# The opening of a two-layer image kernel: order of the first loads, statistics per chunk, and extra TensorE products

## The chip, the cores and the metric

The kernel runs on one core of a Trainium2 chip. The metric is the device time of one execution in microseconds (us); the median of the runs counts. A core has a matrix engine (TensorE, PE in the profile), a vector engine (VectorE, DVE), a scalar engine (ScalarE, ACT), a general engine (GpSimd, POOL) and a queue engine that issues transfers (SyncE, SP). They run side by side and wait for each other by semaphores. Products are written to PSUM banks; all else lies in SBUF, 128 partitions wide.

## What is computed

Two images of 768 channels and 64 x 64 pixels pass through two layers, each with a residual. Each begins with a group norm over 32 groups of 24 channels. The first layer is a state-space block: a projection to 1536 channels, a 3 x 3 convolution per channel, SiLU, a scan over the 4096 pixels, a norm over channels, a projection back. The second is an attention-like block with two projections.

```python
def _gn(v, G=32, eps=1e-5):
    B_, C_, H_, W_ = v.shape
    g = v.reshape(B_, G, C_ // G, H_, W_)
    m = jnp.mean(g, axis=(2, 3, 4), keepdims=True)
    s = jnp.var(g, axis=(2, 3, 4), keepdims=True)
    return ((g - m) / jnp.sqrt(s + eps)).reshape(v.shape)
...
x = x + _L0_conv_ref(_gn(x), ...)
x = x + _L1_conv_ref(_gn(x), L1_conv_W_qkv, L1_conv_W_out, L1_conv_temp)
```

The change touches the group norms, above all that of image 0, with which the kernel begins. All data are float32.

## The kernel before, in words

The order of the instructions of each engine is written out by hand (`manual_schedule`); an engine executes its own in that order, and SP issues its transfers in order too, so that one that waits holds up all behind it.

**The opening (L1156 to L1180).** The constants are issued first: `ident` (L1492), `pc`, `comb`, `xsum` (L80 to L84). Then image 0 is loaded in 48 pieces of 128 channels x 512 pixels, 256 KB each (`gn_load`, L149), and DVE takes the statistics of each (`bn_stats`, L154). Six chunks of 128 channels have eight pieces each; `gn_aggregate` (L231) joins them into a mean and a variance per channel after the last piece.

The channels of a group lie in different partitions, so `gn_parts` joins them on PE. `average` (L188) multiplies the six chunks by six averaging matrices of 128 x 32 and adds up in PSUM: one value per group. `groups` (L193) copies it out, `spread_groups` (L198) multiplies it by six selecting matrices of 32 x 128, one for each chunk: back to one value per channel. This is done twice, for the means and for the variances about them (`deviations`, L204 to L207, between), then `variance` and `end` form the scale (L210 to L214) and `then` the bias (L237, L238). The averaging matrices (`gavg_in`, L170) and the selecting ones (`gsel_in`, L176, two transfers) are loaded into tiles taken from a list of free tiles, `slots`, served in order (`take`, `give`).

The same functions serve image 1 (run in the main loop), and layer 1's group norms of both images (`gn_next`): parts of image 0's stand in the main loop, those of image 1's in the product phase of layer 1 (`beside`), where the weights are loaded by L876 and multiplied by L886.

Behind the statistics of image 0, SP issues: the two matrices, the first tile of x (L307, six), the weights of the first `in_proj` (L323), a first row of x (L337), two more weights, 24 pieces of image 1, `xp_w`, `dt_w`, `pick`. When the scale is there, DVE norms the row (`norm_x0`, L341) and ACT the tile (`norm_x`, L317).

**The filling.** Then come 16 steps. Step n computes on PE, in the first twelve, one row of 64 pixels (`row0`, L348, six products of 128 x 64), and in all 512 pixels (`in_proj`, L362, six products of 128 x 512) for a block of 128 of the 1536 channels, with a weight block (L323) loaded two steps ahead; there are four weight tiles. ACT copies the row out (`carry`, L349) and the rest (`in_proj_evict`, L374 to L377) to one of two buffers `xs`, which DVE reads two steps later for the convolution (`taps_dve`, L461). `row0` writes a PSUM bank of which there is one (`pz`), so it waits until ACT has copied the row before out (L349). ACT writes a buffer `xs` only after DVE has read what was in it. In the same steps DVE takes the statistics of the last 24 pieces of image 1 (`xg`). The taps of the first block stand on DVE behind the first two of those.

**After it** the main loop of 192 steps runs the scan on DVE beside `in_proj` and `out_proj` (L603) on PE, and layer 1 follows.

PE's first product (`acc_mark`, L135) writes the bank `acc` once from `ident` and a zeroed buffer.

Of the kernel before, what the change touches and what calls it, by code (L numbers as in the profile page):

```python
# [7 lines left out]
F32 = mybir.dt.float32  # L8
AF = mybir.ActivationFunctionType
ALU = mybir.AluOpType  # L10
# [4 lines left out]
P = 128  # L15
NB, DM, H, W = 2, 768, 64, 64
L = H * W
# [4 lines left out]
KM = DM // P  # L22
KI = DI // P
G = 32
GC = DM // G
HEADS = 12
HD = DM // HEADS
EPS = 1e-5


TR = 8
# [26 lines left out]
N_MORE = 33  # L58

N_TAIL = 4 * KM  # L60


XD2 = 64
# [2 lines left out]

@with_exitstack
def both_layers(
    ctx, tc, nc, consts, x, in_wP, xp_wP, dt_wP, out_wT, pc_in, comb_in, pick_in, xsum_in, gavg_in, gsel_in, wo_dr, bc_dr, s_dr, x1, stats1,
    qkvP, woutP, temp_c, hcol_in, hsel_in, esel_in, out  # L70
):
    ident, ones, eps_c = consts

    wp = ctx.enter_context(tc.tile_pool(name="l0w", bufs=1))

# [1 line left out]
    r0 = right.enter_context(tc.tile_pool(name="l0r", bufs=1, side="right"))  # L77

    pc = wp.tile([P, KI, PC_N], F32, name="pc")
    nc.sync.dma_start(pc, pc_in)  # L80
    comb = wp.tile([P, 2, P], F32, name="comb")
    nc.sync.dma_start(comb, comb_in)
    xsum = r0.tile([P, XM], F32, name="xsum")
    nc.sync.dma_start(xsum, xsum_in)  # L84
    xp_w = r0.tile([P, KI, XD2], F32, name="xp_w")
    dt_w = r0.tile([XM, KI // 2, P], F32, name="dt_w")
    neg_a = r0.tile([P, KI, NS], F32, name="neg_a")
# [3 lines left out]

    xv = [x[b].rearrange("(k p) h w -> p k (h w)", p=P) for b in range(NB)]
    gp = ctx.enter_context(tc.tile_pool(name="l0gn", bufs=1))
    st_in = [gp.tile([P, KM, L // 512, 6], F32, name="st_in")] * NB
    mv_in = [gp.tile([P, KM, 2], F32, name=f"mv_in{b}") for b in range(NB)]

# [15 lines left out]
    def take():  # L112
        return slots.pop(0)
# [17 lines left out]
    psS = ctx.enter_context(tc.tile_pool(name="l0_pss", bufs=1, space=PSUM))  # L131


    acc = psC.tile([P, 512], F32, tag="acc", name="acc_mark")
    nc.tensor.matmul(acc, ident, xs_bufs[0][:, :TR, :W], start=True, stop=True)  # L135


    pieces = {}
# [3 lines left out]
    def gn_load(b, v):  # L142
        k, h = divmod(v, L // 512)
        if v < N_EARLY[b]:
            pieces[b, v] = take()
        else:
            tag, bufs = (("delta", 3), ("sq", 3), ("du", 2))[v % 8 // 3]
            pieces[b, v] = wk.tile([P, 512], F32, tag=tag, name=f"xg{b}_{v}", bufs=bufs)
        nc.sync.dma_start(pieces[b, v], xv[b][:, k, h * 512 : (h + 1) * 512])  # L149

    def gn_piece(b, v):
        k, h = divmod(v, L // 512)
        piece = pieces.pop((b, v))
        nc.vector.bn_stats(st_in[b][:, k, h, :], piece)  # L154
        if v < N_EARLY[b]:
            give(piece)

    def gn_parts(name, mv, mean, rstd, then, keep=False):

        st, held = {}, {"avg": [], "sel": []}

        def load(what):
            if what in st:
                return
            if what == "avg":
                held["avg"] = [take()]
                st["avg"] = held["avg"][0][:, : KM * G].rearrange("p (k g) -> p k g", g=G)
                nc.sync.dma_start(st["avg"], gavg_in)  # L170
            else:
                held["sel"] = [take(), take()]
                st["sel"] = []
                for h, t in enumerate(held["sel"]):
                    t = t[:G, : KM // 2 * P].rearrange("g (k p) -> g k p", p=P)
                    nc.sync.dma_start(t, gsel_in[:, h * (KM // 2) : (h + 1) * (KM // 2), :])  # L176
                    st["sel"] += [t[:, k, :] for k in range(KM // 2)]

        def done(what):
            if not keep:  # L180
                st.pop(what)
                for t in held[what]:
                    give(t)

        def average(src):
            st["ps"] = psZ.tile([P, 512], F32, tag="pz", name=f"pg_{name}")
            for k in range(KM):
                nc.tensor.matmul(st["ps"][:G, 0:1], st["avg"][:, k, :], src[:, k : k + 1], start=(k == 0), stop=(k == KM - 1))  # L188
            done("avg")

        def groups():
            st["gs"] = gp.tile([G, 1], F32, tag="gn_g", name=f"gs_{name}")
            nc.vector.tensor_copy(st["gs"], st["ps"][:G, 0:1])  # L193

        def spread_groups():
            st["ps"] = psZ.tile([P, 512], F32, tag="pz", name=f"pb_{name}")
            for k in range(KM):
                nc.tensor.matmul(st["ps"][:, k : k + 1], st["sel"][k], st["gs"], start=True, stop=True)  # L198
            done("sel")

        d = gp.tile([P, KM], F32, tag="gn_d", name=f"d_{name}")

        def deviations():
            nc.vector.tensor_copy(mean, st["ps"][:, :KM])  # L204
            nc.vector.tensor_sub(d, mv[:, :, 0], mean)
            nc.vector.tensor_mul(d, d, d)
            nc.vector.tensor_add(d, d, mv[:, :, 1])  # L207

        def variance():
            nc.vector.tensor_scalar_add(d, st["ps"][:, :KM], EPS)  # L210
            nc.scalar.activation(d, d, AF.Sqrt)

        def end():
            nc.vector.reciprocal(rstd, d)  # L214
            then()
            if keep:
                for t in held["avg"] + held["sel"]:
                    give(t)

        nothing = lambda: None  # L220
        return [
            (lambda: load("avg"), lambda: average(mv[:, :, 0]), groups),
            (lambda: load("sel"), spread_groups, deviations),
            (lambda: load("avg"), lambda: average(d), groups),
            (lambda: load("sel"), spread_groups, variance),
            (nothing, nothing, end),
        ]

    def gn_aggregate(b):
        for k in range(KM):  # L230
            nc.vector.bn_aggr(mv_in[b][:, k, :], st_in[b][:, k, :, :])  # L231

    def gn_finish(b):
        mean = gp.tile([P, KM], F32, name=f"xmean{b}")

        def then():
            nc.vector.tensor_mul(xbias[b], mean, xscale[b])  # L237
            nc.vector.tensor_scalar_mul(xbias[b], xbias[b], -1.0)  # L238
            nc.vector.tensor_scalar_mul(stats1[b][:, :, 2 * NT], mv_in[b][:, :, 0], -1.0)

        return gn_parts(f"x{b}", mv_in[b], mean, xscale[b], then, keep=(b == 0))
# [79 lines left out]
    def load_wi(n):  # L321
        w = take_w(KM)
        nc.sync.dma_start(w, in_wP[n % KI])  # L323
        wis[n] = w
# [14 lines left out]
    def norm_x0():  # L339
        for k in range(KM):  # L340
            nc.vector.tensor_scalar(  # L341
                x0s[0][:, k, :], x0s[0][:, k, :], xscale[0][:, k : k + 1], xbias[0][:, k : k + 1], ALU.mult, ALU.add
            )
# [811 lines left out]
    with tc.manual_schedule():  # L1155
        for v in range(N_PIECE):  # L1156
            gn_load(0, v)
            gn_piece(0, v)
        gn_aggregate(0)
        parts = gn_finish(0)  # L1160
        for load, pe, dve in parts[:2]:
            load()
# [3 lines left out]
        load_x0()  # L1166
        for n in (1, 2):
            load_wi(n)
        for v in range(N_EARLY[1]):
            gn_load(1, v)  # L1170
        nc.sync.dma_start(xp_w, xp_wP)
        nc.sync.dma_start(dt_w, dt_wP)
        for load, pe, dve in parts:
            pe()
            dve()
        norm_x0()
        for k in range(KM):
            norm_x(0, k)
# [300 lines left out]

@with_exitstack  # L1480
def mamba_then_attention(
    ctx, tc, x, in_wP, xp_wP, dt_wP, out_wT, pc_in, comb_in, pick_in, xsum_in, qkvP, woutP, temp_c, ident_in, gavg_in, gsel_in, hcol_in, hsel_in, esel_in, out
):
    nc = tc.nc
    keep = ctx.enter_context(tc.tile_pool(name="keep", bufs=1))
    dram = ctx.enter_context(tc.tile_pool(name="dram", bufs=1, space=DRAM))
    x1 = [dram.tile([DM, L], F32, name=f"x1_{b}") for b in range(NB)]

    stats1 = [keep.tile([P, KM, 2 * NT + 1], F32, name=f"stats1_{b}") for b in range(NB)]

    ident = keep.tile([P, P], F32, name="ident")
    nc.sync.dma_start(ident, ident_in)  # L1492
    ones = keep.tile([P, P], F32, name="ones")
    nc.vector.memset(ones, 1.0)
    eps_c = keep.tile([P, 1], F32, name="eps_c")
    nc.vector.memset(eps_c, EPS)
    consts = (ident, ones, eps_c)


    wo_dr = dram.tile([KM // 2, KI // 3, P, 3, 2 * P], F32, name="wo_dr")  # L1500
    bc_dr = [dram.tile([2 * NS, TL], F32, name=f"bc_dr{i}") for i in range(NI)]

    s_dr = {k: dram.tile([KM // 2, 4, P, KM // 2, P], F32, name=f"s_dr_{k}") for k in ("p1", "p3")}
    both_layers(
        tc, nc, consts, x, in_wP, xp_wP, dt_wP, out_wT, pc_in, comb_in, pick_in, xsum_in, gavg_in, gsel_in, wo_dr, bc_dr, s_dr, x1, stats1,
        qkvP, woutP, temp_c, hcol_in, hsel_in, esel_in, [out[b].rearrange("c h w -> c (h w)") for b in range(NB)],
    )

# [104 lines left out]
```

## Time and profile before

| | us |
|---|---|
| median of three runs | 3709.17 |
| lowest, highest | 3702.92, 3709.97 |
| span of the profiled execution | 3708.1 |
| PE busy in it | 3555.3 (96%) |
| DVE busy | 2842.1 (77%) |
| ACT busy | 2571.8 (69%) |
| POOL busy | 1782.8 (48%) |

Of the profiled execution the span is known, from its first instruction to its last; the median of the timed runs is 1.07 us above it. The profile lists instructions by engine with their line in the kernel, the tile that is written and those that are read, and what ended the idle time ahead of each. PE is the matrix engine's products, PEld its loads of weights, SPq the issues of transfers. Times in the timeline are counted from the span's start.

### The profile page before, as it was taken

To read this page: it belongs to the slowest core of one execution; us is meant where nothing else is said; L and a number is where in the kernel's file an instruction comes from. 1 tells how busy PE (TensorE), PEld (TensorE's weight loads), DVE (VectorE), ACT (ScalarE), POOL (GpSimd) and SP (SyncE) were. 2 spreads that over 40 slices of the span, in tenths; PEclk is the share of its full clock that TensorE was granted. 3 is DMA by queue.
4 is the path that set the end of the run, shared out by engine and by line. 5 is a ranking of instruction groups with operands and counts; after the bars stand their busy time and mean duration, and the time that the engine had idled before them with its cause. 6 is when DMAs were issued, how large, how long until landed. Compare 5 with 4: busy or idle time off the path is not lost. (4 is left out here: it accounts for less than half of the span.)

```text
span 3708.1 us, 37935 instructions
## 1 busy us (share of the span) xinstructions
PE 3555.3 (96%) x11176; PEld 1771.0 (48%) x11176; DVE 2842.1 (77%) x2571; ACT 2571.8 (69%) x5026; POOL 1782.8 (48%) x1813
## 2 busy tenths in 40 slices
PE   5968999999999999999999999999999999999999
PEld 3423333343333333333344333433347658886688
DVE  7899999999999999999999999997721362224522
ACT  2688889888988898888888988897633542244221
POOL 0355565565655655555556655654443313330232
PEclk9978999999999999999999999999999999999999
DMA  9877888998989899898898989997676538763487
GB/s 354 232 169 162 182 204 185 205 211 191 212 176 209 201 200 208 184 204 185 187 203 194 212 175 211 203 201 177 142 202 183 192 93 265 256 205 123 158 268 245
DMA packets 380301, 738.98 MB, mean 199 GB/s; under 512 B 44304, under 2 KB 116944, under 8 KB 376000
## 3 DMA queue, kind: packets, MB, share of 16 engines
q0 software_dynamic: 146208, 270.08, 42.6%
q1 hardware_dynamic: 233888, 466.49, 38.4%
q8 instruction: 90, 1.47, 0.2%
q14 instruction: 115, 0.94, 0.1%
HBM read 440.96 MB, written 60.03 MB: 135 GB/s over the span
## 5 line engine op out<-in xcount | busy, mean ns | idle before, releaser
L362 PE MATMUL pa<-u,w 128*128 128x512 f32 (+1 forms) x2304 | 1035.8, 599 | 7.5 <-ACT carry L377 7.3
L603 PE MATMUL po<-u,w 128*128 128x512 f32 x2256 | 1011.5, 598 | 8.1 <-DVE u L615 7.9
L539 DVE TENSOR_TENSOR_SCAN s<-da,s 128x2052 f32<-128x2052 f32 x192 | 851.1, 4433 | 19.5 <-DVE s L537 0.9
L362 PEld LDWEIGHTS pa<-u,w 128*128 128x128 f32 x2304 | 429.5, 192 | 597.7 <-issue 484.7
L603 PEld LDWEIGHTS po<-u,w 128*128 128x128 f32 x2256 | 420.8, 190 | 582.7 <-issue 551.3
L526 POOL TENSOR_TENSOR ysum<-da 128x1024 f32<-128x1024 f32 x192 | 386.8, 2015 | 547.4 <-DVE da L546 464.1
L461 DVE SCALAR_TENSOR_TENSOR acc<-xs,pc,acc 128x512 f32<-128x512 f32 x698 | 525.6, 753 | 29.2 <-ACT acc L415 12.7
L537 DVE TENSOR_TENSOR s<-du,bc 128x2048 f32<-128x2048 f32 x192 | 439.2, 2288 | 83.0 <-POOL du L518 73.8
L433 POOL DMA_DIRECT2D tm<-tm x309 | 270.3, 875 | 462.7 <-ACT tm L427 423.5
L514 ACT ACTIVATE da<-dl,neg_a 128x512 f32<-128x512 f32 x768 | 489.6, 713 | 0.0
L546 DVE TENSOR_TENSOR da<-s,bc 128x2048 f32<-128x2048 f32 x192 | 440.0, 2292 | 6.3
L533 POOL DMA_DIRECT2D u<-ysum x384 | 380.4, 1255 | 4.2 <-issue 3.5
L427 ACT ACTIVATE tm<-xs,pc 128x512 f32<-128x512 f32 x486 | 317.1, 717 | 15.1 <-DMA tm<-tm 7.3
L415 ACT ACTIVATE acc<-xs,pc 128x512 f32<-128x512 f32 x192 | 132.2, 688 | 215.7 <-DVE u L461 206.4
L518 POOL TENSOR_TENSOR du<-dl,u 128x512 f32<-128x512 f32 x192 | 246.5, 1284 | 0.0
L439 POOL DMA_DIRECT2D u<-tm x177 | 206.1, 1164 | 59.6 <-issue 50.1
L447 PE MATMUL acc<-xs,dg 128*128 128x512 f32 x264 | 140.0, 641 | 50.0 <-ACT acc L415 49.6
L886 PE MATMUL po_p<-v,w 128*128 128x256 f32 x672 | 171.9, 380 | 1.4 <-ACT po_p L983 1.4
L886 PE MATMUL po_p<-u,w 128*128 128x256 f32 x624 | 159.7, 379 | 0.0
L461 DVE SCALAR_TENSOR_TENSOR u<-xs,pc,acc 128x512 f32<-128x512 f32 x192 | 143.6, 748 | 7.7
L831 POOL TENSOR_TENSOR v<-u 128x256 f32<-128x256 f32 x21 | 15.7, 758 | 277.1 <-ACT u L849 262.1
L886 PE MATMUL acc_p<-u,w 128*128 128x256 f32 x556 | 143.7, 382 | 4.6 <-DMA w<-woutP 3.4
(285 smaller groups left out, 5006.5 us busy)
## 6 DMA issues: line engine op xcount, KB each, us to landing
u<-ysum POOLq DMA_DIRECT2D x384, 256.0 KB, 5.5
tm<-tm POOLq DMA_DIRECT2D x309, 256.0 KB, 4.3
w<-in_wP SPq DMA_DIRECT2D x192, 384.0 KB, 4.4
w<-wo_dr SPq DMA_DIRECT2D x192, 384.0 KB, 4.7
u<-x SPq DMA_DIRECT2D x263, 256.0 KB, 4.8
w<-s_dr_p SPq DMA_DIRECT2D x288, 192.0 KB, 3.4
u<-tm POOLq DMA_DIRECT2D x177, 256.0 KB, 5.8
bc<-bc_dr SPq DMA_DIRECT2D x32, 1024.0 KB, 7.7
```

The lines of the kernel that those rows point to most:

```text
L362: nc.tensor.matmul(pa[:, :nn], w[:, k, :], xts[i, k][:, :nn], start=(k == 0), stop=(k == KM - 1))
L427: nc.scalar.activation(tm.rearrange("p (h w) -> p h w", w=W), xs[:, dy : dy + TR, dx : dx + W], AF.Copy, scale=pc[:, c, PC_W + j : PC_W + ...
L433: nc.gpsimd.dma_start(tms[a][0], tms[a][q], accum_op=ALU.add)
L461: nc.vector.scalar_tensor_tensor(dst, xs[:, dy : dy + TR, dx : dx + W], pc[:, c, PC_W + j : PC_W + j + 1], acc, ALU.mult, ALU.add)
L514: nc.scalar.activation(das[g % 2][:, n, 1:], deltas[g], AF.Exp, scale=neg_a[:, c, n : n + 1])
L526: nc.gpsimd.tensor_add(ysum[:, 0 : 2 + g % 2 : 1 + g % 2, :], da[:, 0:2, 1:], da[:, 2:4, 1:])
L533: nc.gpsimd.dma_start(us[g], ysums(g, n), accum_op=ALU.add)
L537: nc.vector.tensor_mul(s[:, :, 1:], dus.pop(g).unsqueeze(1).to_broadcast([P, NS, TL]), bc[:, :NS, :])
L539: nc.vector.tensor_tensor_scan(sf, das[g % 2].rearrange("p n l -> p (n l)"), sf, 0.0, ALU.mult, ALU.add)
L546: nc.vector.tensor_mul(das[g % 2][:, :, 1:], s[:, :, 1:], bc[:, NS:, :])
L603: nc.tensor.matmul(po[e], w[:, kk, e * P : (e + 1) * P], us[i * KI + k], start=(k == 0), stop=(k == KI - 1))
L886: nc.tensor.matmul(dst, half[:, k, :], tiles[blocks[seq[i][0]][:3]][what][k], start=(start and k == 0), stop=(k == KH - 1), skip_group_che ...
```

## The change

1. The four constants leave the front of SP's queue. `ident` and `comb`, and a new one, `ghalf` (32 x 2), are issued behind the ninth piece; `pc` behind the weights of the first three steps; `xsum` behind the 24 pieces of image 1.
2. Each chunk of image 0 is aggregated as soon as its eighth piece has its statistics.
3. PE gets products whose result nobody reads: `warm` multiplies `ident` by `comb` (128 x 256) into the bank `acc`; `warm_behind` does so behind a product that reads the statistics of one of the last ten pieces of image 0. One more `warm` stands behind the first spread, two behind the second, and `mark`, the former first product, behind the last part of the norm.
4. A value per group is spread by three matrices of 32 x 128 instead of six: the channel chunks k and k+3 have the same pattern, with groups shifted by 16, so a moving operand of two columns (`ghalf` masks one half of the groups in each) gives both. One transfer of `gsel_in` instead of two, one tile taken instead of two. This holds for all four group norms.
5. The bias of layer 0's norms is one instruction instead of two.

```diff
+    def warm(n=1):
+        acc = psC.tile([P, 512], F32, tag="acc", name="acc_warm")
+        for _ in range(n):
+            nc.tensor.matmul(acc[:, : 2 * P], ident, comb.rearrange("p e m -> p (e m)"), start=True, stop=True)
+
+    def warm_behind(b, k, h):
+        acc = psC.tile([P, 512], F32, tag="acc", name="acc_behind")
+        nc.tensor.matmul(acc[:, :6], ident, st_in[b][:, k, h, :], start=True, stop=True)
+        warm()
+
+    def mark():
+        acc = psC.tile([P, 512], F32, tag="acc", name="acc_mark")
+        nc.tensor.matmul(acc, ident, xs_bufs[0][:, :TR, :W], start=True, stop=True)
...
-                held["sel"] = [take(), take()]
...
+                held["sel"] = [take()]
+                st["sel"] = held["sel"][0][:G, : KM // 2 * P].rearrange("g (k p) -> g k p", p=P)
+                nc.sync.dma_start(st["sel"], gsel_in)
...
-            nc.vector.tensor_copy(st["gs"], st["ps"][:G, 0:1])
+            st["gs"] = gp.tile([G, 2], F32, tag="gn_g", name=f"gs_{name}")
+            nc.vector.tensor_mul(st["gs"], st["ps"][:G, 0:1].to_broadcast([G, 2]), ghalf)
...
-            for k in range(KM):
-                nc.tensor.matmul(st["ps"][:, k : k + 1], st["sel"][k], st["gs"], start=True, stop=True)
+            for k in range(KM // 2):
+                nc.tensor.matmul(st["ps"][:, 2 * k : 2 * k + 2], st["sel"][:, k, :], st["gs"], start=True, stop=True)
...
-            nc.vector.tensor_copy(mean, st["ps"][:, :KM])
+            nc.vector.tensor_copy(chunks(mean), by_chunk())
...
-            nc.vector.tensor_scalar_add(d, st["ps"][:, :KM], EPS)
+            nc.vector.tensor_scalar_add(chunks(d), by_chunk(), EPS)
...
-            nc.vector.tensor_mul(xbias[b], mean, xscale[b])
-            nc.vector.tensor_scalar_mul(xbias[b], xbias[b], -1.0)
+            nc.vector.scalar_tensor_tensor(xbias[b], mean, -1.0, xscale[b], ALU.mult, ALU.mult)
...
         for v in range(N_PIECE):
             gn_load(0, v)
+            if v == 8:
+                nc.sync.dma_start(ident, ident_in)
+                nc.sync.dma_start(comb, comb_in)
+                nc.sync.dma_start(ghalf, ghalf_in)
             gn_piece(0, v)
-        gn_aggregate(0)
+            k, h = divmod(v, L // 512)
+            if h == L // 512 - 1:
+                nc.vector.bn_aggr(mv_in[0][:, k, :], st_in[0][:, k, :, :])
+            if v >= N_PIECE - N_WARM:
+                warm_behind(0, k, h)
...
+        nc.sync.dma_start(pc, pc_in)
         for v in range(N_EARLY[1]):
             gn_load(1, v)
+        nc.sync.dma_start(xsum, xsum_in)
         nc.sync.dma_start(xp_w, xp_wP)
         nc.sync.dma_start(dt_w, dt_wP)
-        for load, pe, dve in parts:
+        for q, (load, pe, dve) in enumerate(parts):
             pe()
+            warm((0, 1, 0, 2, 0)[q])
             dve()
+        mark()
         norm_x0()
```

## The prediction

> **What bounds the kernel.** The table by engine came first (PE 3555.3 of 3708.1 us), then the timeline of the first 90 us, where nearly all of the change lies, then the three later group norms. fp32 products are recorded as two instructions each ("halves"), so x12 is six products. In the timeline (start, duration, engine, line, operation, count, idle before it and what ended that):
>
> ```profile
> 2.59 31.19 SPq L149 DMA_DIRECT2D u<-x  x48
> 39.26 0.69 DVE L154 BATCH_NORM_STATS2 st_in<-u 128x6 f32<-128x512 f32 x1 [0.42 <-DMA u<-x]
> 39.87 1.51 DVE L231 BATCH_NORM_AGGREGATE mv_in<-st_in 128x2 f32<-128x48 f32 x6
> 41.93 2.72 PE L198 MATMUL pb_x<-gs_x,u 32*128 32x1 f32 x12 [0.24 <-DVE gs_x L193]
> 45.60 0.77 PE L188 MATMUL pg_x<-d_x,u 128*32 128x1 f32 x12 [0.95 <-DVE d_x L207]
> 50.84 2.79 PE L348 MATMUL pa<-u,w 128*128 128x64 f32 x12 [1.52 <-issue]
> 53.43 6.74 PE L362 MATMUL pa<-u,w 128*128 128x512 f32 x12
> 60.01 1.45 PE L348 MATMUL pa<-u,w 128*128 128x64 f32 x12
> 64.24 0.33 SPq L323 DMA_DIRECT2D w<-in_wP  x1
> 69.92 1.36 DVE L154 BATCH_NORM_STATS2 st_in<-xg 128x6 f32<-128x512 f32 x2 [2.49 <-DMA xg<-x]
> 72.98 1.45 PE L348 MATMUL pa<-u,w 128*128 128x64 f32 x12
> 75.97 0.59 ACT L375 COPY xs<-pa 128x512 f32<-128x512 f32 x1 [2.05 <-DVE u L461]
> 77.85 0.21 ACT L349 COPY carry<-pa 128x64 f32<-128x64 f32 x1
> 79.47 1.45 PE L348 MATMUL pa<-u,w 128*128 128x64 f32 x12
> ```
>
> Until 39.3 us DVE works at the pace of the pieces; from 39.9 to 50.8 a chain between PE and DVE stands alone; from 53.4 PE is without a gap, one step every 6.48 us. But the transfers are full as well: the table by stretches has 380 to 400 GB/s in every slice of 2 us from 12 to 62 but two (251 at 38, 324 at 44), and the first two pieces of image 1 that are loaded in steps reach DVE only at 69.92, after 2.49 us of idle. What the start gains is worth only what the transfers behind it let through.
>
> **The clock.** PE halves its pace when it was idle: L348 takes 2.79 at 50.84 and 1.45 at 60.01; twelve halves of L198 take 2.72 here and 1.49 at 1879.05. Two more rows, both of the same product:
>
> ```profile
> 169.39 1.13 PE L502 MATMUL pz<-xd,dt_w 48*128 48x512 f32 x4 [2.06 <-ACT xd L491]
> 170.45 5.42 PE L362 MATMUL pa<-u,w 128*128 128x512 f32 x12
> 178.24 7.11 PE L362 MATMUL pa<-u,w 128*128 128x512 f32 x12 [2.37 <-ACT carry L377]
> ```
>
> After 2.06 us of idle PE is still fast, after 2.37 slow, for 1.7 us in all.
>
> **The change, part by part.** *Pieces first.* Four issues leave the front of SP's queue: the first piece is issued at 0.74 instead of 2.59, 1.85 us earlier. Three small ones come back behind the ninth piece: 0.5 us if only their 192 KB count at 387 GB/s, 1.2 as three issues of 0.4; I take 0.8, so the last piece lands 1.05 us earlier. ident and comb are read first at 32.8, well after. The other two constants only move on: pc is issued behind L323 at about 42, lands 5.4 later (the backlog that pieces show), and its first reader is L1384 at 62.26; xsum's is L486 at 166.31. Both are hidden by 15 us and more, but their bytes, and SP's 0.4 each, stay in the full stream. For image 1 the stream is thus ahead only by what DMA stood idle at the start plus one of two selecting loads: 0.8 us (0.3 to 1.3).
>
> *Aggregates per chunk.* Statistics cost 0.60 (22 in 13.16 at 51.78) at a pace of 0.68 per piece, which leaves 0.64 per eight pieces for one aggregate of 0.25 to 0.31: hidden; without that cover 1.25 would come back. The last ends at 39.26+0.69-1.05+0.31 = 39.2 instead of 41.38: 2.2 earlier.
>
> *Ten sets of extra products,* from piece 38 on, stand in PE's queue ahead of the averages. No such set is in the trace. From a half with 128 columns of weights at 0.11 fast and 0.22 slow (L348: 1.31 and 2.63 for twelve) and a half of 256 columns at 0.215 and 0.43 (half of L362's spacing), with one load of weights hidden, a set is 0.65 fast and 1.3 slow, against a piece every 0.68. Piece 38's statistics end at 38.9 - 9 x 0.68 = 32.8; PE falls behind until the clock turns. In this trace it turned at about 56.1, 2.7 us after L362 began and 5.3 after L348 began. With x us of slow work the sets end at 32.8 + x + (10 - x/1.3) x 0.65 = 39.3 + x/2: 40.7 to 42.0, taken as 41.3. So the averages end at 41.8 (0.5 fast, as 0.54 at 1791.96) where they ended at 41.70: the whole gain of the two parts above goes into warming PE. The Trainium skill, TensorE: Matmul & The Clock Gate (Part 1: The HAM clock gate), states that the clock rises after one busy window of 3.4 us, the windows free-running; by an estimate from that page the slow time is 3.4 to 6.8, and the sets would end at 41.0 to 42.7 instead.
>
> *Three spreading matrices, warm.* The chain from the average to L317 took 41.73 to 50.43 = 8.70. Two spreads of 2.72 become six fast halves of 0.7 each: -4.0; the second average 0.77 to 0.54: -0.2; one DVE instruction fewer (L238): -0.2. The product in L193 and the strided copies replace copies of 0.15: nothing. So norming starts at 41.8+8.7-4.4 = 46.1 instead of 50.43. One filler (0.43) fits beside the deviations (0.8). Two fillers and the moved mark (0.86+0.86) against a wait of 1.3 put the first L348 0.4 later, behind norm_x0's own 1.43: hidden; slow, they are 3.4 and not hidden. L348 then ends near 48.4, and L362, fast from its start (5.15), near 53.5: the first in_proj is done **6.5 us earlier** than at 60.01.
>
> *What receives it.* Two things stand in the way, each with a slack: (1) the fourth in_wP block, issued at 64.24 behind the two pieces that land at 69.9; 384 KB at 387 GB/s more make it land near 70.9, with 0.8 taken off 70.1. PE would ask for it at 72.98-6.5 = 66.5. (2) L348 at 79.47 needs the bank that L349 empties at 78.06; L349 stands on ACT behind L375, which waits for DVE's taps, which wait for the pieces of 69.92: slack 1.4, with 0.8 together 2.2. So PE idles 3.6 us at (1), more than the 2.37 that made it slow, and pays 1.75 again (7.11 against 5.37): at 79.47 it is 2.9-1.75 = 1.1 us ahead (bounds: 2.2 if the clock holds; -0.3 at a penalty of 3.2, what L502 with 2.08 and L362 with 7.72 lose after the 2.7 us of idle at 1800). The same page of the Trainium skill (Why this matters for your kernels) has the clock drop only after gaps of over some 3 us, where the row has 2.37; by its rule 3.6 is just enough, and the term the same. Behind this point DVE runs 5.5 us a step against PE's 6.48 and catches up, so 1.1 is kept.
>
> *The other group norms.* Image 1's stands where DVE never waits over 0.32 us (250 to 345): nothing. Layer 1's first has two spreads of 1.49 on a PE without gaps, 0.7 saved each; DVE is nearly as full there, so half: 0.7 (0 to 1.4). Layer 1's second is on the path:
>
> ```profile
> 2833.41 0.89 SPq L176 DMA_DIRECT2D u<-gsel_in  x2
> 2839.11 2.72 PE L198 MATMUL pb_y<-gs_y,u 32*128 32x1 f32 x12 [3.77 <-DMA u<-gsel_in]
> 2862.27 1.49 PE L198 MATMUL pb_y<-gs_y,u 32*128 32x1 f32 x12
> ```
>
> One issue fewer brings the selecting load 0.45 earlier; the spreads save 0.7 each (the first 1.4 if its slow stretch shrinks with it): 1.9 (1.4 to 3.2).
>
> Sum: 1.1+0.7+1.9 = **3.7 us** (1.1 to 6.8) off the profiled 3708.1. The median of the runs is 1.07 above that span, so 3709.2-3.7 = **3705.5**, own range 3702.4 to 3708.1. 0.2% (7.4 us) is about what a measurement of this kernel can tell from no change.
>
> **Rivals.** *B, the start passes whole:* the block of (1) isn't needed to land in that order (its landing is worked out, not recorded), or the stream gets ahead with the pieces. 6.5+0.7+1.9 = 9.1: 3700.1. For it: no row shows PE waiting for in_wP; against it: 2.49 us of DVE waiting at 69.92.
> *C, the fillers don't raise the clock:* their halves leave PE loading weights a third of the time. Ten sets at 1.3 end at 45.8, the slow average at 46.6, the chain takes 6.1, two slow fillers and the mark push L348 to 55.2 instead of 50.84. +4.4-2.6 = +1.8: 3711.0, slower. It decides as soon as the clock has not turned by 45 us. Against it: PE is busy without a break from 32.8.
> *D, another order of buffers:* one selecting tile instead of two moves every later take() by one slot, and a load that waits for a slot's last reader holds all of SP's queue. The price is at 3186.36:
>
> ```profile
> 3186.36 2.90 PE L886 MATMUL acc_p<-u,w 128*128 128x256 f32 x6 [3.38 <-DMA w<-woutP]
> ```
>
> 3.38 of waiting and 1.5 of slow clock, 5 us. One such stall more eats the forecast's gain, three make 3720.5, beyond the 0.2%. Against it: the list is served in order and longer by one.
>
> **How the numbers follow.** Forecast 0.46 (0.04 of it beyond 0.2% faster, by runs that scatter from 3702.92 to 3709.97), B 0.31 (0.30 faster, 0.01 within), C 0.09 (0.07 within, 0.02 slower), D 0.14 (0.02 within, 0.12 slower). Faster 0.34, within 0.52, slower 0.14. The range runs from 3697.5, under B, to 3712, over C, and leaves out most of D.
>
> **What would show it.** First piece issued at 0.74; last aggregate near 39.2; the sets still running at 41; L198 at 0.7 twice; first L317 near 46; PE idle 3 to 4 us ahead of the fourth step's L348 near 70, then slow; that L348's successor about 1 us ahead of 79.47. Wrong if the gap is missing (B), if L362 starts slow (C), or if new DMA waits stand behind 2900 us (D).

## The result and the profile after

The changed kernel takes 3714.12 us (median of 17 runs, 3707.11 to 3719.82), the one before, on the same chip, 3707.95 (17 runs, 3699.91 to 3710.64): ratio **1.0018, 95% interval 1.0012 to 1.0024**, so 4.4 to 8.9 us slower. The profiled spans are 3708.1 and 3712.3. The forecast was 3705.5, in a range up to 3712.0.

The timeline of the changed kernel's opening, in the columns used above:

```profile
0.74 4.34 SPq L159 DMA_DIRECT2D u<-x  x9
33.56 0.59 PE L140 MATMUL acc_behind<-st_in,ident 128*128 128x6 f32 x2 [33.56 <-DVE st_in L164]
34.21 1.22 PE L136 MATMUL acc_warm<-comb,ident 128*128 128x256 f32 x2
35.49 0.50 PEld L140 LDWEIGHTS acc_behind<-st_in,ident 128*128 128x128 f32 x2 [0.78 <-PE acc_warm L136]
35.49 0.60 PE L140 MATMUL acc_behind<-st_in,ident 128*128 128x6 f32 x2
...
39.83 0.37 DVE L1177 BATCH_NORM_AGGREGATE mv_in<-st_in 128x2 f32<-128x48 f32 x1
...
51.61 1.22 PE L136 MATMUL acc_warm<-comb,ident 128*128 128x256 f32 x2
52.76 0.80 PE L195 MATMUL pg_x<-mv_in,u 128*32 128x1 f32 x12
53.80 1.44 PE L205 MATMUL pb_x<-gs_x,u 32*128 32x2 f32 x6 [0.24 <-DVE gs_x L200]
...
58.73 1.35 PEld L136 LDWEIGHTS acc_warm<-comb,ident 128*128 128x128 f32 x4
58.73 2.08 PE L136 MATMUL acc_warm<-comb,ident 128*128 128x256 f32 x4
60.96 1.95 PE L145 MATMUL acc_mark<-xs,ident 128*128 128x512 f32 x2
62.74 1.45 PE L360 MATMUL pa<-u,w 128*128 128x64 f32 x12
64.02 5.37 PE L374 MATMUL pa<-u,w 128*128 128x512 f32 x12
69.23 1.45 PE L360 MATMUL pa<-u,w 128*128 128x64 f32 x12
76.70 3.91 DVE L473 SCALAR_TENSOR_TENSOR acc<-xs,pc,acc 128x512 f32<-128x512 f32 x5
```

The last aggregate is done at 40.20, 1.18 earlier than before (41.38). The ten sets stand on PE from 33.56 to 52.8, with gaps of under 0.1 us and without ever getting faster: each is 1.93 us from start to start. So the average, which needs the aggregate and stands behind them in PE's order, begins at 52.76, 12.6 us after the aggregate was there. The chain behind is at the slow pace too (0.80, 1.44, where the forecast had 0.54, 0.7). The clock rises only at 62.7, and the second row product (L360; L348 before) stands at 69.23 instead of 60.01. DVE's first tap sum (L473; L461 before) follows at 76.70 instead of 71.20; in the main loop the fifth scan runs 6.9 us behind the first profile of before, and the span ends 4.2 later.

### The profile page after: what moved, and what is told of

Read it like the earlier page. It is cut to its first block, busy times and chain, and to the rows that moved or that the text cites. A ratio compares the mean times of both kernels' runs of the same rounds, so it can differ in the third digit from the quotient of the medians.

```text
span 3712.3 us, 37915 instructions
## 1 busy us (share of the span) xinstructions
PE 3561.7 (96%) x11174; PEld 1772.6 (48%) x11174; DVE 2841.8 (77%) x2569; ACT 2570.4 (69%) x5026; POOL 1780.5 (48%) x1813
## 5 line engine op out<-in xcount | busy, mean ns | idle before, releaser
L473 DVE SCALAR_TENSOR_TENSOR acc<-xs,pc,acc 128x512 f32<-128x512 f32 x698 | 525.9, 753 | 31.7 <-ACT acc L427 15.0
L451 POOL DMA_DIRECT2D u<-tm x177 | 205.8, 1163 | 55.9 <-issue 38.9
L898 PE MATMUL po_p<-u,w 128*128 128x256 f32 x690 | 178.7, 382 | 0.0
L898 PE MATMUL po_p<-v,w 128*128 128x256 f32 x606 | 157.9, 380 | 1.6 <-ACT po_p L995 1.4
L473 DVE SCALAR_TENSOR_TENSOR u<-xs,pc,acc 128x512 f32<-128x512 f32 x192 | 143.6, 748 | 7.7
L387 ACT COPY xs<-pa 128x512 f32<-128x512 f32 (+1 forms) x192 | 109.7, 571 | 49.5 <-PE pa L374 48.3
L898 PEld LDWEIGHTS po_p<-u,w 128*128 128x128 f32 x690 | 132.6, 192 | 18.4
```

Source lines behind the costliest of these rows:

```text
L473: nc.vector.scalar_tensor_tensor(dst, xs[:, dy : dy + TR, dx : dx + W], pc[:, c, PC_W + j : PC_W + j + 1], acc, ALU.mult, ALU.add)
L898: nc.tensor.matmul(dst, half[:, k, :], tiles[blocks[seq[i][0]][:3]][what][k], start=(start and k == 0), stop=(k == KH - 1), skip_group_che ...
```

## The experiments

Thirteen variants beside the changed kernel and the one before, of which there are two profiles. In this section S is the theory that the sets are the loss, as a queue of slow products that never warms PE. The table has, from the one profile of each, the start of the first average, of the second row product, of the first tap sum on DVE, and the fifth scan of the main loop against the second profile of the kernel before (`e0_before`); then the ratio of the run times to those of the kernel before on the same chip, with its 95% interval (the quotient of the two medians lies up to 0.0008 off it, in e6). All other times are from the span's start.

| kernel | average | row 2 | tap sum | scan 5 | ratio, interval |
|---|---|---|---|---|---|
| before, first profile | 40.28 | 60.01 | 71.20 | +0.67 | 1 |
| before, second profile | 40.78 | 60.21 | 71.19 | 0 | 1 |
| changed | 52.76 | 69.23 | 76.70 | +7.58 | 1.0018 [1.0012, 1.0024] |
| e1, no extra products | 39.73 | 57.49 | 70.44 | -3.23 | 0.9973 [0.9963, 0.9983] |
| e2, three matrices alone | 40.27 | 58.27 | 69.96 | -2.16 | 0.9977 [0.9969, 0.9986] |
| e8, the same, two buffers | 40.23 | 58.46 | 70.31 | -1.28 | 0.9976 [0.9967, 0.9985] |
| e7, order and aggregates alone | 38.51 | 58.20 | 70.03 | -3.08 | 0.9994 [0.9984, 1.0003] |
| e6, fillers without sets | 39.00 | 55.92 | 71.06 | +2.24 | 0.9984 [0.9975, 0.9992] |
| e10, five sets | 43.35 | 59.99 | 71.35 | -0.47 | 0.9990 [0.9978, 1.0001] |
| e13, sets of 6 columns | 41.22 | 59.99 | 70.97 | 0.00 | 0.9985 [0.9976, 0.9994] |
| e12, sets of 256 columns | 45.55 | 62.34 | 70.81 | +2.83 | 0.9998 [0.9988, 1.0008] |
| e4, sets on random data | 51.32 | 70.68 | 75.26 | +9.35 | one run, 3717.03 us |
| e3, 512 columns instead | 41.04 | 58.65 | 70.51 | -1.59 | 0.9993 [0.9984, 1.0002] |
| e5, 512 columns of zeros | 40.83 | 56.51 | 70.81 | -1.55 | one run, 3701.30 us |
| e9, e6 and an early block | 40.26 | 57.26 | 74.00 | +4.41 | 0.9992 [0.9983, 1.0001] |
| e11, e1 and an early block | 39.81 | 57.14 | 71.71 | +0.16 | 0.9985 [0.9975, 0.9994] |

### Which part of the change costs

**e1: no extra products.** Edit to the changed kernel:

```diff
-            if v >= N_PIECE - N_WARM:
-                warm_behind(0, k, h)
...
-            warm((0, 1, 0, 2, 0)[q])
```

> The changed kernel without any of the extra products (no sets behind the last ten pieces, no fillers in the norm; the mark stays behind the norm). Theory Q (the sets stand slow in PE's queue and hold back the first average): the first average starts right behind the last aggregate, near 40.3 us instead of 52.76, norming near 46.4, the first in_proj (slow) ends near 56 instead of 69.2. Behind it the fourth block of weights and the row's bank take part of the lead, so that the fifth row starts 1.3 to 2.2 us ahead of 79.47. Ratio to the kernel before 0.9985 to 0.9990. Rival (the loss lies elsewhere, in the moved constants or the order of buffers): the ratio stays above 1.001.

Its timeline:

```profile
39.73 1.01 PE L195 MATMUL pg_x<-mv_in,u 128*32 128x1 f32 x12 [39.73 <-DMA u<-gavg_in]
40.97 1.44 PE L205 MATMUL pb_x<-gs_x,u 32*128 32x2 f32 x6 [0.24 <-DVE gs_x L200]
45.73 2.08 PE L145 MATMUL acc_mark<-xs,ident 128*128 128x512 f32 x2
47.60 2.66 PE L360 MATMUL pa<-u,w 128*128 128x64 f32 x12
57.49 1.45 PE L360 MATMUL pa<-u,w 128*128 128x64 f32 x12
69.16 1.36 DVE L164 BATCH_NORM_STATS2 st_in<-xg 128x6 f32<-128x512 f32 x2 [3.12 <-DMA xg<-x]
70.93 1.52 PE L360 MATMUL pa<-u,w 128*128 128x64 f32 x12 [0.29 <-DMA w<-in_wP]
77.50 1.45 PE L360 MATMUL pa<-u,w 128*128 128x64 f32 x12
```

The whole chain runs cold, and yet the second row product is 2.5 us earlier than before and 11.7 earlier than in the changed kernel. 0.9973 (expected 0.9985 to 0.9990) against 1.0018: by these the extra products cost about 17 us (0.45% of 3708), and what is left of the change is a gain of 6 to 14 us. At 70.93 the fourth row product waits for the fourth weight block, as the forecast's first receiver says, and the fifth is 1.97 ahead of 79.47.

**e2: three matrices alone,** the kernel before with change 4 (`ghalf` issued behind the ninth piece) and nothing else.

> The kernel before with the three spreading matrices alone (ghalf loaded behind the ninth piece; all else as before). Both theories: two spreads of 1.4 instead of 2.72 in image 0's norm, so the first in_proj ends 2.7 us earlier, near 57.3; the row's bank lets 1.4 of it through; layer 1's second norm saves 1.9. Ratio 0.9988 to 0.9993. If the order of buffers costs something, it shows here: ratio 1.000 or above.

The spreads take 1.43 and 1.44, cold, for 2.72 each, and 8.5 us are gained at the end, by 0.9977 where 0.9988 to 0.9993 was expected. The start explains about two of them.

**e8** gives each spreading two buffers again, `held["sel"] = [take(), take()]`, so that the order of the buffers is that of before.

> The kernel before with the three spreading matrices, but each spreading holds two buffers as before (the second is taken and not used), so that the order of the buffers stays the one of before. If the 9 us of three matrices come from the matrices (start 1.7, the norms after it), the ratio is 0.9972 to 0.9984 again (0.9977 with one buffer). If more than half came from the freed buffer and the new order of slots, the ratio is 0.9987 or more, and the small early steps of the scans (0.8 at 442, 0.8 at 507, 0.9 at 1135, 1.2 at 1621 us) are missing from the trace.

0.9976: the buffer and its order are not it, the matrices are. (Of the small steps that the expectation names, see `e0_before`.)

**e7: order of the first loads and aggregates per chunk alone,** the kernel before with changes 1 (without `ghalf`) and 2, and `mark()` behind the norm.

> The kernel before with one part of the change: pieces ahead of the constants, aggregates per chunk, the mark behind the norm; six spreading matrices stay and there are no extra products. Theory S: the first average stands near 39.7 (before 42.1), the second row product 1.5 to 2.5 ahead of 60.01, the fifth row product at 77.5 to 78.2 (79.47 before) because the fourth weight block holds it, and the ratio is 0.9985 to 0.9996 if the later gains of the kernel with three matrices belong to the matrices; 0.9973 to 0.9980, the same as with both parts, if they do not and any start that comes early takes the same gains with it.

The average begins at 38.51, 1.8 earlier, the fifth row product at 77.67 (expected 77.5 to 78.2). At the end 2.2 us are left, and the interval holds 1.

**e0: the kernel before, unchanged, a second profile.**

> The kernel before once more, unchanged, for a second profile. If the steps at 442, 507, 574, 600, 1135 and 1621 us that every variant shows against the first profile are gains of the variants, this profile lies within 0.3 us of the first one at each of them; if they are stalls of that one execution, this profile has them too, and its scans run 4 us ahead of the first by 1650 us. The same for the clock's drop at 1800 to 1807 and the second norm of the second stage.

Both, in part. Of the six steps those at 442 (0.76), 1135 (0.89) and 1621 (1.19) are in this profile as in nearly all the others: there the first execution had stalled, and no variant gains anything. At 507 it has 0.20 of 0.76, at 574 and 600 nothing. The first execution's drop of the clock at 1800, worth 3.3 us, is not in this one either. Two profiles of one kernel lie up to 6 us apart in the middle (at 1930) and 0.3 at the end.

**e6: fillers without the sets.** Only the two lines of `warm_behind` are taken out of the changed kernel.

> The changed kernel without the ten sets behind the last pieces, but with its three fillers in the chain (one behind the first spreading, two behind the second). Only products whose results nobody reads are left out. Theory S (the sets are the loss: ten of 1.93 us at the slow clock, 33.6 to 52.7): the first average stands at 39.7 again as without any extra product, the fillers at the slow clock (1.2 each) put the second average back by 0.3 and the mark by 2.4 to 2.7, and the second row product stands at 58.0 to 60.2 (57.49 without any extra, 69.23 in the changed kernel); ratio 0.9973 to 0.9985. Rival (it is the fillers and the mark inside the chain that cost, the sets end under the statistics): the second row product stays within 3 us of 69.2 and the ratio at 1.001 or more.

Its timeline:

```profile
39.00 1.01 PE L195 MATMUL pg_x<-mv_in,u 128*32 128x1 f32 x12 [39.00 <-DMA u<-gavg_in]
45.17 2.08 PE L136 MATMUL acc_warm<-comb,ident 128*128 128x256 f32 x4
49.24 1.64 PE L360 MATMUL pa<-u,w 128*128 128x64 f32 x12
55.92 1.45 PE L360 MATMUL pa<-u,w 128*128 128x64 f32 x12
72.69 2.05 PE L360 MATMUL pa<-u,w 128*128 128x64 f32 x12 [3.63 <-DMA w<-in_wP]
80.93 1.45 PE L360 MATMUL pa<-u,w 128*128 128x64 f32 x12
```

Taking the sets away is worth 1.0018 - 0.9984, some 12.6 us; the fillers cost the other 4 by the ratios, though the intervals of e6 and e1 overlap. Here the clock rose at 49.6 and the second row product came at 55.92, earlier than the expected 58.0 to 60.2 and than in e1; but the fourth then waits 3.63 us for its weights, PE goes slow again, and the fifth scan is 5.5 us behind e1's. A faster start was turned into a wait and a cold PE.

**e10: five sets,** one behind every second of the last ten pieces (`and v % 2 == 0`).

> The changed kernel with a set behind every second of the last ten pieces, so five sets, and the same fillers. Theory S (sets at the slow clock are a queue of 1.93 us each in front of the first average): the last ends at 43 to 44, the first average stands there (39.0 with none, 52.76 with ten), the second row product at 59 to 63 (55.92 and 69.23), the ratio 0.9988 to 1.0005, between those of none (0.9984) and ten (1.0018). Rival (any set spoils the start, or ten do harm in another way than by their number): the first average stays at 39 to 40 or goes to 50.

The sets end at 43.4, the average follows at 43.35 and row 2 at 59.99, all as expected. Five sets of 1.93 us end at 43.4, ten at 52.8: each set that runs on after the last aggregate is done (near 40) puts the average back by its whole length.

### Why the sets do not raise the clock

**e4** runs the same sets with a piece of the image as weights and moving operand, instead of the unit matrix and constants:

```diff
+        nc.tensor.matmul(acc[:, :6], piece[:, :P], st_in[b][:, k, h, :], start=True, stop=True)
+        nc.tensor.matmul(acc[:, : 2 * P], piece[:, :P], piece[:, 2 * P :], start=True, stop=True)
```

> The changed kernel with the same ten sets, in the same shapes, on dense data: the piece itself stands for ident and for comb. Theory S: nothing changes, a set takes 1.93 us throughout, the first average starts at 52 to 53, the clock turns near 62. Rival Z (zeros don't count): the clock turns 3.4 to 7 us after the first set at 33.6, the sets end near 43 and the first average starts there.

Sets of 1.71 us instead of the expected 1.93, all slow; the average at 51.32. The data are not it. (A set is shorter because its two products write one tile here; see e12.)

**e3: one product of 512 columns behind every second piece,** from the twenty-fifth on, instead of the sets.

```diff
-            if v >= N_PIECE - N_WARM:
-                warm_behind(0, k, h)
+            if v >= 24 and v % 2 == 0:
+                warm_dense(ident, piece)
```

> The changed kernel, the ten sets replaced by twelve products of ident with all 512 columns of every second piece from piece 24 on; the fillers in the norm stay. Theory S (the clock follows the share of time in which columns stream; the sets stream 0.86 of 1.93 us, 44%): the clock turns 3.4 to 7 us after the first of them (near 25), products go from 1.7 to 0.86 us and keep up with the pieces, the first average starts near 40.3 at the full clock, norming near 45, the first in_proj ends 7 us before 60.0. Only 1 to 2.2 of that is left at the fifth row; ratio 0.9985 to 0.9990. Rival Z (products with a matrix that is nearly all zeros don't count): the clock stays slow, twelve products of 1.75 end near 47, ratio 0.9995 to 1.001.

**e5** is the same with the piece as weights and zeros as moving operand.

> The changed kernel with the ten sets replaced by twelve unbroken products behind every second piece from the twenty-fifth on, weights from the piece, the moving operand a tile of zeros; nobody reads the results. Theory S (what raises the clock is how much of the time columns stream, not what they hold): the clock turns near 31 us as with the dense products on the pieces themselves (31.3). Rival Z (zeros do not count as load): no turn before 45 us, the products stay at 1.7 to 2.1 us and the first average comes at 45 or later.

The clock, by the pace of the products, rises at 31.3 (e3, first product at 23.37) and 30.0 (e5, 24.03). The timeline of e5:

```profile
24.03 16.87 PE L145 MATMUL acc_dense<-xs,u 128*128 128x512 f32 x24 [24.03 <-DMA u<-x]
40.83 0.54 PE L199 MATMUL pg_x<-mv_in,u 128*32 128x1 f32 x12
41.61 0.82 PE L209 MATMUL pb_x<-gs_x,u 32*128 32x2 f32 x6 [0.24 <-DVE gs_x L204]
44.21 1.44 PE L209 MATMUL pb_x<-gs_x,u 32*128 32x2 f32 x6 [0.24 <-DVE gs_x L204]
45.58 2.08 PE L136 MATMUL acc_warm<-comb,ident 128*128 128x256 f32 x4
49.58 1.88 PE L364 MATMUL pa<-u,w 128*128 128x64 f32 x12
```

The first half of the chain is as fast as forecast (0.54, 0.82); then the clock falls at 43.7 for 6.8 us (e3: at 45.0 for 10.2) though PE was never idle for more than 0.32 since the last product of 512 columns: what ran in between were products of one or two columns and one filler of 256. So even a set that warms PE leaves the last filler pair, the mark and the first row product cold, in e5 the second spread too, and e3 (0.9993, expected 0.9985 to 0.9990) is no faster than e1 without anything.

**e12: the sets cut to their product of 256 columns,** on the piece itself.

```diff
-                warm_behind(0, k, h)
+                warm_plain(piece)
...
+        nc.tensor.matmul(acc[:, : 2 * P], ident, piece[:, : 2 * P], start=True, stop=True)
```

> The changed kernel with each of the ten sets cut to its one product of 256 columns, which reads the piece itself; the product of 6 columns that read the statistics is gone. Nobody reads the results. Theory S1 (the product of 6 columns, 0.59 us of loading weights in each 1.93, is what keeps the clock down): with products of 256 columns back to back the clock turns 4 to 8 us after the first (before 42 us), the first average takes 0.54 and stands at 40 to 42. Theory S2 (256 columns behind each load of weights are not enough, only 512 are): no turn ahead of the averages, ten products of 1.2 to 1.3 from about 33 on, the first average at 44 to 46, slow (0.8 or more), the second row product at 60 to 64.

Its timeline, the line that decides and the two behind it:

```profile
32.88 12.74 PE L145 MATMUL acc_plain<-u,ident 128*128 128x256 f32 x20 [32.88 <-DMA u<-x]
45.55 0.80 PE L199 MATMUL pg_x<-mv_in,u 128*32 128x1 f32 x12
46.59 1.44 PE L209 MATMUL pb_x<-gs_x,u 32*128 32x2 f32 x6 [0.24 <-DVE gs_x L204]
```

12.74 us for ten products, 0.64 for a half, no turn: the expectation S2. The product of 6 columns is not to blame; products of 256 columns, issued like this, are not enough. How they are issued matters, and the loads of weights show it:

```profile
35.44 0.50 PEld L145 LDWEIGHTS acc_plain<-u,ident 128*128 128x128 f32 x2 [0.78 <-PE acc_plain L145]
```

Each call takes the one bank `acc` as a new tile, so the load of the next product waits 0.78 us for the product before; the changed kernel's sets have the same wait (35.49 in its timeline). Where two products write one tile, there is none: of the changed kernel's two fillers in a row (58.73) the first takes 1.22, both together 2.08, so the second adds 0.86, against 1.27 for a product of e12. In e4 the second product of a set starts 0.45 behind the first, in the changed kernel 0.65. No run has ten products of 256 columns without this wait, so whether those would raise the clock is open. The table by stretches shows what tells the three apart (from:to, length, then PE busy and PEld busy in us, with their counts; the row's clock column reads 1.00 here and can't be used, because the granted clock is recorded only from its first rise on). The changed kernel during its sets, e12 and e5 in theirs:

```profile
34.00:44.00 10.00, 9.36 (x22) 5.21 (x22) 5.97 (x11) 0.00 (x0) 0.00 (x0) 1.00 1.06 368
```

```profile
33.00:45.00 12.00, 11.48 (x20) 4.88 (x20) 7.04 (x12) 0.00 (x0) 0.00 (x0) 1.00 1.06 362
```

```profile
24.00:30.00 6.00, 5.85 (x6) 1.51 (x6) 5.97 (x11) 0.00 (x0) 0.00 (x0) 1.00 1.05 387
```

PE is recorded as busy for 94 to 98% in all three. But loading weights fills 52% of the changed kernel's sets, 41% of e12's, and 25% of e5's, the only ones of the three that raised the clock. With 0.86 us for 256 columns at the slow pace, an estimate of the share of the time in which columns stream is 45% (0.86 of 1.93), 67% (0.86 of 1.27) and 81% (1.72 of the 2.12 from one of e5's products to the next). Three points do not say where the limit lies, nor whether it is the loads or the columns that count.

**e13: the sets cut to the product of 6 columns.**

> The changed kernel with each of the ten sets cut to the product of 6 columns that reads the statistics (0.59 us in the changed kernel, under the pace of the pieces, 0.68 to 0.73); the product of 256 columns is gone there, the fillers in the chain stay. Theory S (a queue of slow work ahead of the averages is the whole loss): no queue builds up, the first average stands at 39.5 to 41 as without sets (39.0), the second row product at 55.5 to 57.5, the ratio 0.9978 to 0.9992. Rival (the tie to the statistics or any product ahead of the averages does the harm): the first average at 44 or later, the ratio 1.0005 or more.

No queue: the average at 41.22, a trifle above the expected 39.5 to 41, the ratio 0.9985 as expected. Row 2 is at 59.99 and not at 55.5 to 57.5, because the clock rose only at 55.9 here, 6.5 us after the mark began; in e6, with the same fillers, mark and row product, it had risen at 49.6, 2.2 us after. Whether three fillers do so in time is not decided by their number.

### What receives the start

**e9 and e11: the fourth weight block ahead of the pieces of image 1,** in e6 and in e1: `for n in (1, 2, 3): load_wi(n)`.

> The changed kernel without its ten sets but with its fillers, and the fourth weight block of in_proj issued ahead of the 24 pieces of image 1. In the run with fillers the second row product stood at 55.92, ahead of the one without any extra product (57.49), but the fourth waited 3.63 us for that block to 72.69 and the first scan came 6 us later. Theory C (that block takes back what the start gains): the fourth row product stands at 68.9 to 69.5, the fifth at 75.4 to 77.5 (80.93), the first scan 3 to 6 us earlier than 194.4, the ratio 0.9960 to 0.9977. Rival (something else holds the fill: the row bank, the pieces of image 1): the fourth row product moves but the first scan moves by less than 1.5 us, and the ratio stays at 0.9984.

> No extra products and the fourth weight block issued ahead of the pieces of image 1. Without the early block the fourth row product waited 0.29 us for it, at 70.93. Theory C: nothing more than 0.3 to 0.6 us to gain there, and the ratio is that of no extra products (0.9973) within 0.0006. Rival (the block holds more of the fill than that wait shows): 0.9965 or lower. Slower than 0.9980 would say that the later pieces of image 1 cost more than the block gives.

The timeline of e11:

```profile
70.12 1.45 PE L360 MATMUL pa<-u,w 128*128 128x64 f32 x12
70.43 1.36 DVE L164 BATCH_NORM_STATS2 st_in<-xg 128x6 f32<-128x512 f32 x2 [3.22 <-DMA xg<-x]
71.71 3.90 DVE L473 SCALAR_TENSOR_TENSOR acc<-xs,pc,acc 128x512 f32<-128x512 f32 x5
78.36 0.21 ACT L361 COPY carry<-pa 128x64 f32<-128x64 f32 x1
78.62 1.55 PE L360 MATMUL pa<-u,w 128*128 128x64 f32 x12 [1.85 <-ACT carry L361]
```

The wait for the block is gone and the fourth row product is 0.8 earlier (70.12); the fifth waits 1.85 for the bank that L361 empties, and is 1.1 later than in e1. The block's bytes stand ahead of image 1's, so the two stepped pieces are read at 70.43 instead of 69.16. In e9 the same wait is 4.03 us, the tap sums come at 74.00, and the fifth row product at 80.92 instead of the expected 75.4 to 77.5. Neither kernel gained (0.9992 and 0.9985, against 0.9984 and 0.9973 without the early block), so theory C fails in both, although the wait that it names is real: the transfers are full (the prediction's table by stretches), and to put one forward is to put another back.

## Why the prediction was wrong, step by step

**The step that failed** is "With x us of slow work the sets end at 39.3 + x/2: 40.7 to 42.0", with x from 2.7 to 5.3. It took the time that PE had worked before the clock rose at 56.1 in the kernel before, the last 2.7 us of it on products of 512 columns, and used it for sets of 6 and 256 columns. PE was slow for all 19.2 us of the sets; in e12 products of 256 columns alone did not raise the clock either, in e3 and e5 products of 512 did. The other term of the same sum, 1.3 us for a slow set "with one load of weights hidden", was 1.93: each product waits for the bank `acc`, and its load is not hidden. Ten sets of 1.93 from 33.56 end at 52.9. From there all that was to be warm was cold: spreads 1.44 for 0.7, fillers and mark slow, row 2 9.2 us later instead of 6.5 earlier. The argument against rival C, "PE is busy without a break from 32.8", was the mistake itself: PE is recorded as busy for 94% of a stretch of which loads of weights fill 52%. The Trainium skill, TensorE: Matmul & The Clock Gate (Part 1: The HAM clock gate), says that whatever is issued in the first 3.4 us or so runs slow and everything after fast; e12's 12.74 us without a turn speak against it for such products.

**Rival C had the mechanism, and one term too small.** Its 1.3 for a set is 0.44 for the product of 6 columns and 0.86 for that of 256, and the runs show both where nothing waits for the bank (0.45 in e4, 0.86 for the second of two fillers). In the sets it is 0.65 and 1.28. Ten make 19.3 instead of 13.0, and the average begins at 52.76 instead of 45.8. Its test, no turn by 45 us, was met. It had the first L348 at 55.2, 4.4 later than before; that product stands at 62.74, 11.9 later, and 6.3 of the 7.5 us between are this term.

**Pieces first, aggregates:** forecast 2.2 earlier at the last aggregate, measured 1.18 in the changed kernel; in e7 the average begins 1.8 to 2.3 earlier than in the two profiles of before. Right in kind.

**The receivers** were right in kind. The fourth block lets e1's row product go at 70.93 (forecast near 70.1); at the fifth 1.97 us were through (forecast 1.1, bounds -0.3 to 2.2), with the clock holding. e6, whose second row product is 4.1 us early, has the forecast wait (3.63, forecast 3.6) and the slow clock behind it, but the block came only at 72.69, and the fifth row product at 80.93 is 1.5 later than before, outside the bounds. With the block early the row bank took its place (e11). Rival B falls with them. The changed kernel itself has no such wait, because its start is late.

**The other norms.** Image 1's: against the first profile the scans shift by 0.03 us at most from 245 to 347 in the changed kernel, e1, e2, e6, e7 and e8; nothing, as forecast. Layer 1's first: forecast 0.7, nothing found; from 1767 to 1936 the changed kernel, e1, e6 and e8 take 4.0 us less than the first profile, and so does e7 with six matrices; the second profile takes 3.6 less. That is the first execution's own drop of the clock at 1800. The same stretch in the other nine variants lies between 4.0 us less and 2.1 more than in the first profile, so that a gain of 0.7 cannot be seen there. Layer 1's second, in the changed kernel:

```profile
2842.38 1.41 PE L205 MATMUL pb_y<-gs_y,u 32*128 32x2 f32 x6 [3.75 <-DMA u<-gsel_in]
2864.78 0.82 PE L205 MATMUL pb_y<-gs_y,u 32*128 32x2 f32 x6
```

2.72 and 1.49 became 1.41 and 0.82, 1.98 us, close to the forecast 1.9. The gain at the end is larger. Fitted over the eleven kernels with three matrices that have a ratio, the time by that ratio moves by 1.2 us per us of the fifth scan, and stands 5.3 us below the kernel before at an unmoved start (single ones scatter by some 2.5 about the line). From the last scan (2700) to 3280 the thirteen profiles with three matrices take 6.5 us less than the second profile on average (2.7 to 9.9), the two others with six 0.4 and 3.5 less: a difference of the means of about 5. Some 2 of it are the spreads; the rest lies around waits for weights near 3186 and 3218, which differ between profiles (3.38 and 2.56 before, 3.08 and 1.74 in e1). Why three matrices should shorten those is open.

**Rival D** falls: e2 and e8 differ by one buffer, and by 0.0001 in the ratio.

**The sum.** By the ratios: three matrices -8.5 us, order and aggregates -2.2, both -10.0 (e1), with the fillers -5.9, with the sets +6.7. e1 beats the kernel before by 0.17 to 0.37% and the changed kernel by about 0.45%.

## What to carry to other kernels

Extra products did not warm PE here while columns streamed for 45 or 67% of their time (estimates), and did at 81%: take one load of weights for as many columns as a product allows, see whether the load of the next waits for the bank of the last, and look for the fall in the duration of one and the same instruction, not for a busy engine. Put nothing in front of a chain on the critical path that, should it stay slow, takes longer than the work it waits for anyway; work out that case first. And before an opening is made faster, look at which transfer the stage behind it waits for: here a start that was 4 us faster ended in a wait of 3.6 us.

## What the runs showed of the hardware

- PE stayed at half pace through 19.2 us of products with gaps of under 0.1 us (52% of the time weight loads, 256 columns at most) and through 12.7 us with 41% loads; it was at full pace 6 to 8 us after the start of products of 512 columns with 25% loads. Which data they held did not matter: 512 columns raised the clock with zeros (e5) as with image data (e3), the sets did not with constants or with image data (e4).
- The clock fell, at 43.7 and 45.0 us, 2.8 and 3.9 us after the last product of 512 columns, while PE worked on products of one and two columns and one filler, with gaps of at most 0.32 us. The Trainium skill, TensorE: Matmul & The Clock Gate (Why this matters for your kernels), has gaps of over some 3 us as the cause; here the clock fell without one.
- The same gap does and does not lower the clock. The first and the second profile of the kernel before, one line of each timeline:

```profile
1800.54 2.08 PE L502 MATMUL pz<-xd,dt_w 48*128 48x512 f32 x4 [2.69 <-DVE gs_y L193]
```

```profile
1797.99 1.13 PE L502 MATMUL pz<-xd,dt_w 48*128 48x512 f32 x4 [2.69 <-DVE gs_y L193]
```

The same instruction behind the same 2.69 us of idle takes 2.08 in the one and 1.13 in the other; the scans show 3.3 us for it. A single profile can thus lie some us off for no reason in the kernel.
- At the slow pace a load of weights was hidden behind a product of 256 columns where the next product did not wait for the bank, and not where it did: the second of two fillers on one tile adds 0.86 us, each of e12's products, whose load waits 0.78 us for the one before, takes 1.27.
